# A new opening for a conditioned attention kernel: order of loads and transposes, and seven-product projections for batch 0

## The chip, the cores and the metric

The kernel runs on one core of a Trainium2 chip. A core has a matrix engine (TensorE, "PE" in the profile), a vector engine (VectorE, DVE), a scalar engine (ScalarE, ACT), GpSimd (POOL) and a queue engine (SyncE, SP). Each executes its own instructions in order; semaphores tie them together. Matmul results land in PSUM, which has eight banks of 128 partitions by 512 float32; all else is kept in SBUF. Data moves between memory and SBUF by DMA, issued here from SP and ACT.

The metric is the device time of one execution, in microseconds; less is better. "PEld" in the profile is the loading of a matmul's stationary operand, which overlaps other matmuls.

## The reference

Self-attention over `x` (8 batches, 512 rows, 512 columns, float32) with 16 heads of 32 columns. A condition row per batch goes through the Q and K projections too and is added to every row's Q and K. The result is added to `x`.

```python
Q = split_heads(x @ Wq.T + bq);  K = split_heads(x @ Wk.T + bk);  V = split_heads(x @ Wv.T + bv)
tQ = split_heads(tokens @ Wq.T + bq);  tK = split_heads(tokens @ Wk.T + bk)   # tokens = cond[:, None, :]
scores = einsum('bhqd,bhkd->bhqk', Q + tQ, K + tK) / sqrt(32)
attn = softmax(scores, axis=-1)
out = x + merge_heads(einsum('bhqk,bhkd->bhqd', attn, V))
```

All arithmetic is float32, and a float32 matmul shows in the trace as two passes (so four matmuls of a projection are listed as x8).

## The kernel before

**Tiling.** The four heads that share 128 columns form a *group*. There are four groups a batch and 32 in all, numbered `t` from 0. A group's Q and K are kept transposed, 128 columns (partitions) by 512 rows, in `qkT`. Rows come in four chunks of 128.

**Work on one group.** For each of four chunks, `row_max` makes the scores of the chunk's 128 rows for the four heads (`row_scores`, L419, into four banks), and DVE takes their maxima in two instructions (L428). `denominators` then lets ACT take the exponential of each of those four banks with the maximum as bias, and sum it (L456): four instructions. When all four chunks have their maxima, `split_max` (POOL) splits them into three bfloat16 parts and `transpose_max` turns them (L482). Only then `exponentials` makes the scores the other way round with the maxima subtracted by a matmul (L498, L501), and ACT writes the weights `e` (L513, L515). `weighted` multiplies them by V (L520), and `output` turns, divides and writes the result.

**The main loop** takes group `t` through four stages, one a chunk. In each stage PE does, in this order: the exponentials' matmuls of group `t`, the row scores of group `t + 1` or `t + 2`, and one piece of other work, among them half a projection for the next batch. It runs 29 times from L720; `advance` moves to the next row of `TURNS`, which says which bank each use has in each stage.

**Two ways to project.** `project_qk` makes one group's Q or K from the turned weight `wT` and the turned input `xT`: four matmuls of 128 by 512 (L255), then one instruction that adds the token's part `tok` and leaves PSUM (DVE for Q, L268; ACT for K, L270). `project_v` does a chunk of V (L281, L288). The other way makes two groups of Q or K, or half of V, at once by seven products of blocks instead of eight (`product`, L321 for V and L324 for Q and K; two matmuls of 128 by 256 each). It needs sums of blocks of the weights (`combine_w`, four POOL instructions for each weight) and of x (`combine_x`, two DVE instructions a half). It comes in halves: `first_products` (products 1, 6, one part of 2, 7) and `other_products` (4, 5, the rest of 2, 3). In `first_products`, product 1 and product 7 go to the two halves of one bank, `one_`, and 6 and 2 to another, `two_`; ACT copies product 1 out as `m1` (L357), and DVE forms sums from it (L364, L365, and `plus`, L344 or L347). The caller hands in `dens`, a function that issues denominators at a fixed place after m1's copy.

**Order.** PE, ACT, DVE and POOL execute in the order in which the program issues (`manual_schedule`); the framework adds the semaphores. DMA issues on SP are in order too. All of PSUM is one tile, cut into banks.

**The opening before.** SP issues the load of the condition, four chunks of x, then Wk, the two biases, the broadcast of bv, and Wv; ACT issues Wq's four chunks and then loads its function table. PE turns each chunk of x (`transpose_x`, L225) and of Wq (`transpose_w`, L180) in turn as they land, projects Q of group 0, does the condition's product for Q (`condition`, L591: product, ACT copy, L593), turns Wk, ends the condition (`condition_end`, L552: four transposes; DVE sums, L600 to L610), projects K of group 0 with the condition's K part inside, and turns half of Wv. Then five `burst_of_maxima` steps follow: row scores, maxima and denominators for a chunk, each with a projection behind it by `project_qk` or `project_v`. In the third to fifth of them the rest of Wv and the chunks of x of batch 1 are turned, and `combine_w` is issued. The projections of batch 0 left over go into the four stages of `t = 0`. So batch 0 is projected without the seven products, batches 1 to 7 with them.

Of the kernel before, what the change touches and what calls it, by code (L numbers as in the profile page):

```python
# [17 lines left out]
def kernel(  # L18
# [33 lines left out]
    nc = tc.nc  # L52
    P = 128
    B, S, D = x.shape
# [5 lines left out]
    NS = S // P  # L60
# [45 lines left out]
    def one():  # L106
        count[0] += 1
        return psum[:, (count[0] - 1) % 8, :]
# [1 line left out]

    xs = {}

    def load_x(n):

        if n < B * NS:
            xs[n] = xp.tile([P, D], F32, tag="x", name=f"x_{n}")
            nc.sync.dma_start(xs[n], x[n // NS, n % NS * P : (n % NS + 1) * P, :])

    xr = {}

# [8 lines left out]
        nc.gpsimd.tensor_tensor(xr[t], xr[t], bias, ALU.add)  # L129

    ws = {}
    for n in ("v", "q", "k"):
        ws[n] = stage.tile([P, NC, D], F32, tag="w", name=f"w_{n}")

    def load_w(n, w, queue):
        wv = w.rearrange("(c p) d -> p c d", p=P)
        for c in range(NC):
            queue.dma_start(ws[n][:, c, :], wv[:, c, :])

    cond_sb = const.tile([B, D], F32, tag="cond", name="cond_sb")  # L140
    nc.sync.dma_start(cond_sb, cond)
    for n in range(NS):
        load_x(n)
    load_w("q", Wq, nc.scalar)
    load_w("k", Wk, nc.sync)
    bqk = const.tile([P, 2, NC], F32, tag="bqk", name="bqk")
    nc.sync.dma_start(bqk[:, 0, :], bq.rearrange("(c p) -> p c", p=P))
    nc.sync.dma_start(bqk[:, 1, :], bk.rearrange("(c p) -> p c", p=P))
# [25 lines left out]
        n: const.tile([P, NC, D], F32, tag=f"wT{n}", name=f"wT_{n}") for n in ("q", "k", "v")  # L174
    }

    def transpose_w(n, dc, pt):

        for cc in range(NC):
            nc.tensor.transpose(  # L180
                pt[:, cc * P : (cc + 1) * P], ws[n][:, dc, cc * P : (cc + 1) * P], ident
            )
        o = wT[n][:, :, dc * P : (dc + 1) * P]
        pv = pt.rearrange("p (c s) -> p c s", c=NC)
        if n == "q":
            if dc % 2:
                nc.vector.tensor_scalar(o, pv, SCALE, None, ALU.mult)
            else:
                nc.scalar.activation(o, pv, AF.Copy, scale=SCALE)
        elif dc % 2:  # L190
            nc.vector.tensor_copy(o, pv)
        else:
            nc.scalar.copy(o, pv)
# [81 lines left out]
            project_qk_part(t, n, cc, pt)  # L275
        project_qk_end(t, n, pt)

    def project_v(n, pt):
        b, sc = divmod(n, NS)
        for cc in range(NC):  # L280
            nc.tensor.matmul(  # L281
                pt,
                xT[b][:, cc, sc * P : (sc + 1) * P],
                wT["v"][:, cc, :],
                start=(cc == 0),
                stop=(cc == NC - 1),
            )
        nc.vector.tensor_copy(vs[b % 2][:, sc, :], pt)  # L288

    MADE_OF = [("11", "11"), ("12", "21"), (3, "22"), ("22", 3), (0, 0), (1, 1), (2, 2)]
# [53 lines left out]
            add = tok[:, "qk".index(n), u * 2 + g, b : b + 1]  # L346
            nc.vector.scalar_tensor_tensor(o, pt, add, rest, ALU.add, ALU.add)  # L347

    def first_products(n, b, u, dens, small, at):

        one_, two_ = banks(0), banks(at)
        c1, c12, c2, c22 = parts_of(n, b, u)
        m1 = c2[:, 0, :]
        product(n, b, u, 1, one_[:, :HS])
        nc.scalar.copy(m1, one_[:, :HS])  # L357
        dens()
        small()
# [264 lines left out]
    warm = one()  # L624
    for _ in range(28):
        nc.tensor.matmul(warm[:, :P], onesb, onesb, start=True, stop=True)
    for c in range(NS):
        transpose_x(c, one())
        transpose_w("q", c, one())
        if c == 1:  # L630
            pc = one()
            for cc in range(NC):
                nc.tensor.transpose(
                    pc[:, cc * B : (cc + 1) * B], cond_sb[:, cc * P : (cc + 1) * P], ident[:B, :B]
                )
            nc.vector.tensor_copy(
                condT[:, :, 0:B], pc[:, : NC * B].rearrange("p (c b) -> p c b", b=B)
            )
    pq = one()
    for cc in range(NC):  # L640
        project_qk_part(0, "q", cc, pq)
    condition("q", one())
    for c in range(NC):
        transpose_w("k", c, one())
    condition_end("q", one())
    project_qk_end(0, "q", pq)
    condition("k", one())
    pk = one()
    for cc in range(NC):
        project_qk_part(0, "k", cc, pk)  # L650
        if cc == 1:
            condition_end("k", one())
    project_qk_end(0, "k", pk)
    transpose_w("v", 0, one())
    transpose_w("v", 1, one())
    turn[0] = 3

    def nothing():
        pass

    def burst_of_maxima(t, qc):
        row_max(t, qc)
        if qc == NS - 1:
            split_max(t)
        denominators(t, qc)

    burst_of_maxima(0, 0)
    project_qk(1, "q", banks(1))
    advance()
    burst_of_maxima(0, 1)  # L670
    project_qk(1, "k", banks(1))
    advance()
    burst_of_maxima(0, 2)
    transpose_w("v", 2, banks(0))
    transpose_w("v", 3, banks(1))
    transpose_x(NS, banks(2))
    project_qk(2, "q", banks(3))
    advance()
    burst_of_maxima(0, 3)
    for n in ("v", "q", "k"):  # L680
        combine_w(n)
    transpose_x(NS + 1, banks(0))
    project_v(0, banks(3))
    transpose_x(NS + 2, banks(1))
    project_qk(2, "k", banks(2))
    advance()
    burst_of_maxima(1, 0)
    project_v(1, banks(3))
    transpose_max(0, banks(1))
    transpose_x(NS + 3, banks(2))  # L690
    project_qk(3, "q", banks(0))
    load_residual(0)
    advance()

# [25 lines left out]
    for t in range(T - 3):  # L720
# [18 lines left out]
        exponentials(t, 1)  # L739
        row_max(t + 1, 2)  # L740
        denominators(t + 1, 2)
        if t:
            invert(t - 1, sums[t - 1])
# [172 lines left out]
```

## Time and profile before

| | |
|---|---|
| median of 3 runs | 767.25 us (766.59 to 768.86) |
| the profiled execution | 767.8 us, of which its span is 766.0 us |
| granted TensorE clock | 0.998 |
| first transposes of x on PE | 5.29 us |
| first projection (L255) | 10.22 us |
| first row scores (L419) | 24.10 us |
| first exponentials' matmul (L498) | 58.43 us |

The span runs from the program's first profiled instruction to its last; what lies around it, 1.8 us here, is in the time and not in the trace. PE is busy nearly throughout, so the profile is best read along PE: the chain of work that ended last names, step by step, what the next step waited for. The other engines matter only where they appear in it.

### The profile page before, as it was taken

Reading aid. Unit: us, or ns where it says so; the run is one execution under the profiler, and the core shown is the slowest. Engines: PE = TensorE matmul, PEld = TensorE weight load, DVE = VectorE, ACT = ScalarE, POOL = GpSimd, SP = SyncE. Lnnn points to the kernel's source line nnn. Section 1 sums busy time; section 2 is a strip of 40 time slices with the busy share of each in tenths; the row PEclk is TensorE's granted clock in tenths of the full one; section 3 lists DMA queues with packets and bytes.
Section 4 is the critical chain, followed back from the end, with each engine's and each line's share of the span. In section 5 each row is a group of like instructions: output and inputs, shape, how many; then the busy total and the mean of one; then the engine's idle time right before and its main releaser. Section 6 shows DMA issues by size and latency. Waiting matters only on the chain.

```text
span 766.0 us, 14203 instructions
## 1 busy us (share of the span) xinstructions
PE 754.7 (99%) x5424; PEld 426.3 (56%) x5424; DVE 521.5 (68%) x720; ACT 627.1 (82%) x1454; POOL 127.3 (17%) x223
## 2 busy tenths in 40 slices
PE   8999999999999999999999999999999999999997
PEld 5444566555656655555655555665555665555332
DVE  4455676676767777677777776777766777667664
ACT  2447898888889888888888888898888988888865
POOL 0063011111011111111111101111110111110220
PEclk9999999999999999999999999999999999999999
DMA  9011011101111110111111011110101101010100
GB/s 305 26 42 29 15 42 42 32 12 45 40 43 42 40 31 15 42 42 43 42 28 43 15 42 42 42 42 11 46 1 29 29 29 28 1 39 18 43 28 28
DMA packets 41571, 29.76 MB, mean 39 GB/s; under 512 B 2840, under 2 KB 35608, under 8 KB 41504
## 3 DMA queue, kind: packets, MB, share of 16 engines
q1 hardware_dynamic: 40656, 27.68, 12.7%
q10 hardware_dynamic: 848, 1.18, 0.5%
q8 instruction: 42, 0.69, 0.4%
q14 instruction: 25, 0.20, 0.1%
HBM read 20.47 MB, written 8.39 MB: 38 GB/s over the span
## 4 chain that ended last, share of the span: by engine, by line
PE 96%; ACT 1%; DVE 1%; DMA 1%; issue 0%; SPq 0%; DVEq 0%
PE psum L324 23%; PE psum L520 15%; PE psum L501 14%; PE psum L419 14%; PE psum L321 12%; PE psum L498 6%; PE psum L255 4%; PE psum L225 2%; PE psum L552 2%; PE psum L281 2%; PE psum L482 1%; DMA x<-in_x_dram 1%; ACT e L513 1%; PE psum L180 1%; ACT e L515 0%
## 5 line engine op out<-in xcount | busy, mean ns | idle before, releaser
L428 DVE TENSOR_REDUCE nmax<-psum 128x2 f32<-128x1024 f32 x256 | 301.7, 1219 | 165.0 <-PE psum L419 164.0
L456 ACT ACTIVATE dead<-psum,nmax 128x512 f32<-128x512 f32 x496 | 335.0, 692 | 23.1 <-DVE nmax L428 23.1
L513 ACT ACTIVATE e<-psum 128x512 f32<-128x512 f32 x270 | 145.8, 595 | 86.6 <-PE psum L501 86.6
L419 PE MATMUL psum<-kT,qT 32*128 32x512 f32 x1024 | 138.9, 598 | 0.3 <-ACT e L515 0.3
L501 PE MATMUL psum<-qT,kT 32*128 32x512 f32 x1024 | 132.7, 589 | 0.0
L515 ACT ACTIVATE e<-psum 128x1024 f32<-128x1024 f32 x121 | 124.7, 1031 | 0.0
L520 PE MATMUL psum<-e,v 128*32 128x512 f32 x1024 | 119.0, 598 | 0.4 <-ACT e L515 0.3
L456 ACT ACTIVATION_READ_ACCUMULATOR dead<-psum,nmax 128x1 f32 x496 | 103.6, 209 | 0.0
L470 POOL CAST split<-nmax 128x16 bf16<-128x16 f32 x32 | 8.2, 255 | 544.2 <-DVE nmax L428 544.2
L419 PEld LDWEIGHTS psum<-kT,qT 32*128 32x128 f32 x1024 | 64.7, 183 | 52.0 <-issue 27.7
L520 PEld LDWEIGHTS psum<-e,v 128*32 128x32 f32 x1024 | 29.6, 110 | 83.2 <-issue 58.2
L498 PE MATMUL psum<-maxT,onesb 3*128 3x512 bf16 x512 | 51.2, 384 | 1.7 <-DVE res L566 0.8
L501 PEld LDWEIGHTS psum<-qT,kT 32*128 32x128 f32 x1024 | 51.1, 185 | 2.5 <-issue 0.2
L577 POOL TENSOR_TENSOR res<-res,xr 128x512 f32<-128x512 f32 x30 | 38.2, 1272 | 66.1 <-DVE res L566 66.1
L498 PEld LDWEIGHTS <-onesb 3*128 3x128 bf16 x512 | 13.3, 91 | 63.6 <-issue 54.1
L542 DVE COPY oT<-psum 128x512 f32<-128x512 f32 x29 | 20.0, 691 | 35.7 <-PE psum L520 35.7
L324 PE MATMUL psum<-xc,wc_q 128*128 128x256 f32 x168 | 43.4, 380 | 0.3 <-ACT e L515 0.3
L321 PE MATMUL psum<-wc_v,xc 128*128 128x256 f32 x168 | 43.2, 380 | 0.0
L324 PE MATMUL psum<-xc,wc_k 128*128 128x256 f32 x168 | 43.2, 380 | 0.0
L129 POOL TENSOR_TENSOR xr<-xr,bvb 128x512 f32<-128x512 f32 x32 | 40.6, 1269 | 0.0
L324 PEld LDWEIGHTS psum<-xT,wT_k 128*128 128x128 f32 x168 | 26.4, 190 | 12.8 <-ACT e L513 10.6
L324 PEld LDWEIGHTS psum<-xc,wc_q 128*128 128x128 f32 x168 | 30.8, 190 | 4.7 <-ACT e L515 1.1
(144 smaller groups left out, 834.1 us busy)
## 6 DMA issues: line engine op xcount, KB each, us to landing
x<-in_x_dram SPq DMA_DIRECT2D x33, 256.0 KB, 2.7
xr<-in_x_dram SPq DMA_DIRECT2D x32, 256.0 KB, 3.1
out_dram<-res SPq DMA_DIRECT2D x31, 256.0 KB, 2.4
w_q<-in_L_cond_Wq_dram ACTq DMA_DIRECT2D x4, 256.0 KB, 4.5
w_k<-in_L_cond_Wk_dram SPq DMA_DIRECT2D x4, 256.0 KB, 4.9
w_v<-in_L_cond_Wv_dram SPq DMA_DIRECT2D x4, 256.0 KB, 6.7
bvb<-in_L_cond_bv_dram SPq DMA_DIRECT2D x1, 256.0 KB, 6.2
out_dram<-res SPq DMA_DIRECT2D x1, 128.0 KB, 1.8
```

Of the source, the lines that this page charges most:

```text
L129: nc.gpsimd.tensor_tensor(xr[t], xr[t], bias, ALU.add)
L321: nc.tensor.matmul(pt, xb, w, start=(kc == kcs[0]), stop=(kc == kcs[-1]))
L324: nc.tensor.matmul(pt, w, xb, start=(kc == kcs[0]), stop=(kc == kcs[-1]))
L419: nc.tensor.matmul(pt, qkT["q", t][r, qc * P : (qc + 1) * P], qkT["k", t][r, :], start=True, stop=True,)
L428: nc.vector.tensor_reduce(nmax[t][:, qc, pr * 2 : pr * 2 + 2, 0], pt, AX.X, ALU.max, negate=True)
L456: nc.scalar.activation(dead, banks(HG + j), AF.Exp, bias=nmax[t][:, qc, j, :], accum_out=sums[t][:, qc, j, :],)
L498: nc.tensor.matmul(bank[j], onesb[r, :], maxT[t][r, :], start=True, stop=False)
L501: nc.tensor.matmul(bank[j], qkT["k", t][r, kc * P : (kc + 1) * P], qkT["q", t][r, :], start=False, stop=True,)
L513: nc.scalar.activation(e[:, i, :], bank[pr * 2 + i], AF.Exp)
L515: nc.scalar.activation(e, banks(2, 2), AF.Exp)
L520: nc.tensor.matmul(pt[j * HD : (j + 1) * HD, :], vs[b % 2][:, kc, (g * HG + j) * HD : (g * HG + j + 1) * HD], es[t, kc, j // 2][:, j % 2, ...
L577: last.tensor_tensor(y, y, xr.pop(t), ALU.add)
```

## The change

It touches the opening, the five burst steps and the four stages of `t = 0`. Nothing else in the kernel is changed.

- Loads: SP issues x_0, Wq's first chunk, x_2, Wq's other chunks, then the condition, the biases, bv's broadcast and Wv. ACT issues x_1, x_3 and Wk's four chunks.
- Transposes: all four chunks of x and the first chunks of Wq and Wk come first, with the two projections of group 0 between them; x's copies out of PSUM alternate between DVE and ACT. `combine_x` for batch 0 follows the Q projection. The other chunks of Wq and Wk come next, then the condition's whole work for both, and all of Wv. `combine_w` is issued as each weight is complete.
- Bursts: the turning of batch 1's chunks of x, and the transposed maxima, go between the maxima and the denominators, with ACT copying. `split_max(0)` moves behind the fourth burst.
- Projections: Q, K of groups 0 and 1 stay as they were; groups 2 and 3 and all of V of batch 0 use `first_products` and `other_products`. `project_v` goes. In the bursts the products come after `denominators` with nothing handed in as `dens`.

```diff
-    def load_x(n):
+    def load_x(n, queue=nc.sync):
...
-    for n in ("v", "q", "k"):
+    for n in ("q", "k", "v"):
         ws[n] = stage.tile([P, NC, D], F32, tag="w", name=f"w_{n}")
...
+    load_x(0)
+    load_x(1, nc.scalar)
+    load_w("q", Wq, nc.sync, [0])
+    load_x(2)
+    load_x(3, nc.scalar)
+    load_w("k", Wk, nc.scalar, [0])
+    load_w("q", Wq, nc.sync, [1, 2, 3])
+    load_w("k", Wk, nc.scalar, [1, 2, 3])
     cond_sb = const.tile([B, D], F32, tag="cond", name="cond_sb")
     nc.sync.dma_start(cond_sb, cond)
-    for n in range(NS):
-        load_x(n)
-    load_w("q", Wq, nc.scalar)
-    load_w("k", Wk, nc.sync)
...
-    def first_products(n, b, u, dens, small, at):
+    def first_products(n, b, u, dens, small, at, first=0):
...
-        one_, two_ = banks(0), banks(at)
+        one_, two_ = banks(first), banks(at)
...
-    for c in range(NS):
-        transpose_x(c, one())
-        transpose_w("q", c, one())
...
-    pq = one()
+    for c, copy in ((0, nc.vector.tensor_copy), (1, nc.scalar.copy)):
+        transpose_x(c, one(), copy)
+    transpose_w("q", 0, one(), 1)
+    for c, copy in ((3, nc.scalar.copy), (2, nc.vector.tensor_copy)):
+        transpose_x(c, one(), copy)
+    pq, pk = one(), one()
+    one_of = [0]
+
+    def other():
+        one_of[0] += 1
+        return psum[:, (one_of[0] - 1) % 5, :]
+
     for cc in range(NC):
         project_qk_part(0, "q", cc, pq)
-    condition("q", one())
-    for c in range(NC):
-        transpose_w("k", c, one())
-    condition_end("q", one())
-    project_qk_end(0, "q", pq)
-    condition("k", one())
-    pk = one()
+    transpose_w("k", 0, other(), 0)
+    combine_x(0, 0)
+    combine_x(0, 1)
     for cc in range(NC):
         project_qk_part(0, "k", cc, pk)
-        if cc == 1:
-            condition_end("k", one())
+    for n in ("q", "k"):
+        for c in range(1, NC):
+            transpose_w(n, c, other(), (c + (n == "k")) % 2)
+        combine_w(n)
+    pc = other()
...
+    condition("q", other())
+    condition("k", other())
+    transpose_w("v", 0, other())
+    transpose_w("v", 1, other())
+    condition_end("q", other())
+    project_qk_end(0, "q", pq)
+    condition_end("k", other())
     project_qk_end(0, "k", pk)
-    transpose_w("v", 0, one())
-    transpose_w("v", 1, one())
+    transpose_w("v", 2, other())
+    transpose_w("v", 3, other())
+    combine_w("v")
     turn[0] = 3
...
-    def burst_of_maxima(t, qc):
+    def burst_of_maxima(t, qc, between=nothing):
+
         row_max(t, qc)
-        if qc == NS - 1:
-            split_max(t)
+        between()
         denominators(t, qc)
 
-    burst_of_maxima(0, 0)
+    burst_of_maxima(0, 0, lambda: transpose_x(NS, banks(0), nc.scalar.copy))
     project_qk(1, "q", banks(1))
     advance()
-    burst_of_maxima(0, 1)
+    burst_of_maxima(0, 1, lambda: transpose_x(NS + 1, banks(0), nc.scalar.copy))
     project_qk(1, "k", banks(1))
     advance()
-    burst_of_maxima(0, 2)
-    transpose_w("v", 2, banks(0))
-    transpose_w("v", 3, banks(1))
-    transpose_x(NS, banks(2))
-    project_qk(2, "q", banks(3))
+    burst_of_maxima(0, 2, lambda: transpose_x(NS + 2, banks(0), nc.scalar.copy))
+    first_products("q", 0, 1, nothing, nothing, 3, 2)
     advance()
     burst_of_maxima(0, 3)
-    for n in ("v", "q", "k"):
-        combine_w(n)
-    transpose_x(NS + 1, banks(0))
-    project_v(0, banks(3))
-    transpose_x(NS + 2, banks(1))
-    project_qk(2, "k", banks(2))
+    split_max(0)
+    other_products("q", 0, 1, nothing, nothing, (0, 3))
+    first_products("v", 0, 0, nothing, nothing, 2, 1)
     advance()
-    burst_of_maxima(1, 0)
-    project_v(1, banks(3))
-    transpose_max(0, banks(1))
-    transpose_x(NS + 3, banks(2))
-    project_qk(3, "q", banks(0))
+    burst_of_maxima(1, 0, lambda: transpose_max(0, banks(2), nc.scalar.copy))
+    first_products("k", 0, 1, nothing, nothing, 1, 3)
+    other_products("v", 0, 0, nothing, nothing, (0, 2))
     load_residual(0)
     advance()
...
-                dens()
-                project_qk(3, "k", banks(1))
+                other_products("k", 0, 1, dens, nothing, (1, 3))
...
-            project_v(2, banks(0))
+            first_products("v", 0, 1, dens, nothing, 1)
...
-            dens()
-            project_v(3, banks(0))
+            other_products("v", 0, 1, dens, nothing, (0, 2))
```

`transpose_w` gets an argument that picks the engine of its copy (DVE if odd, else ACT), and `load_w` one that picks chunks.

More of the change, by code (lines that the diff above doesn't have):

```diff
@@ L111 @@
     xs = {}
-    def load_x(n):
+    def load_x(n, queue=nc.sync):
         if n < B * NS:
             xs[n] = xp.tile([P, D], F32, tag="x", name=f"x_{n}")
-            nc.sync.dma_start(xs[n], x[n // NS, n % NS * P : (n % NS + 1) * P, :])
+            queue.dma_start(xs[n], x[n // NS, n % NS * P : (n % NS + 1) * P, :])
     xr = {}
@@ L131, with load_w @@
     ws = {}
-    for n in ("v", "q", "k"):
+    for n in ("q", "k", "v"):
         ws[n] = stage.tile([P, NC, D], F32, tag="w", name=f"w_{n}")
-    def load_w(n, w, queue):
+    def load_w(n, w, queue, cs=range(NC)):
         wv = w.rearrange("(c p) d -> p c d", p=P)
-        for c in range(NC):
+        for c in cs:
             queue.dma_start(ws[n][:, c, :], wv[:, c, :])
+    load_x(0)
[6 more added lines that the diff above has]
+    load_w("k", Wk, nc.scalar, [1, 2, 3])
     cond_sb = const.tile([B, D], F32, tag="cond", name="cond_sb")
     nc.sync.dma_start(cond_sb, cond)
-    for n in range(NS):
-        load_x(n)
-    load_w("q", Wq, nc.scalar)
-    load_w("k", Wk, nc.sync)
     bqk = const.tile([P, 2, NC], F32, tag="bqk", name="bqk")
@@ L175, with transpose_w @@
     }
-    def transpose_w(n, dc, pt):
+    def transpose_w(n, dc, pt, odd=None):
+        odd = dc % 2 if odd is None else odd
         for cc in range(NC):
@@ L185, in transpose_w @@
         if n == "q":
-            if dc % 2:
+            if odd:
                 nc.vector.tensor_scalar(o, pv, SCALE, None, ALU.mult)
@@ L189, in transpose_w @@
                 nc.scalar.activation(o, pv, AF.Copy, scale=SCALE)
-        elif dc % 2:
+        elif odd:
             nc.vector.tensor_copy(o, pv)
@@ L276, in project_qk @@
         project_qk_end(t, n, pt)
[L278 to L288, printed above, removed]
     MADE_OF = [("11", "11"), ("12", "21"), (3, "22"), ("22", 3), (0, 0), (1, 1), (2, 2)]
@@ L626 @@
         nc.tensor.matmul(warm[:, :P], onesb, onesb, start=True, stop=True)
-    for c in range(NS):
-        transpose_x(c, one())
-        transpose_w("q", c, one())
[L630 to L638, printed above, removed]
-    pq = one()
+    for c, copy in ((0, nc.vector.tensor_copy), (1, nc.scalar.copy)):
[8 more added lines that the diff above has]
+        return psum[:, (one_of[0] - 1) % 5, :]
     for cc in range(NC):
         project_qk_part(0, "q", cc, pq)
-    condition("q", one())
-    for c in range(NC):
-        transpose_w("k", c, one())
-    condition_end("q", one())
-    project_qk_end(0, "q", pq)
-    condition("k", one())
-    pk = one()
+    transpose_w("k", 0, other(), 0)
+    combine_x(0, 0)
+    combine_x(0, 1)
     for cc in range(NC):
         project_qk_part(0, "k", cc, pk)
-        if cc == 1:
-            condition_end("k", one())
+    for n in ("q", "k"):
[3 more added lines that the diff above has]
+    pc = other()
+    for cc in range(NC):
+        nc.tensor.transpose(
+            pc[:, cc * B : (cc + 1) * B], cond_sb[:, cc * P : (cc + 1) * P], ident[:B, :B]
+        )
+    nc.vector.tensor_copy(condT[:, :, 0:B], pc[:, : NC * B].rearrange("p (c b) -> p c b", b=B))
+    condition("q", other())
[5 more added lines that the diff above has]
+    condition_end("k", other())
     project_qk_end(0, "k", pk)
-    transpose_w("v", 0, one())
-    transpose_w("v", 1, one())
+    transpose_w("v", 2, other())
+    transpose_w("v", 3, other())
+    combine_w("v")
     turn[0] = 3
@@ L740 @@
         row_max(t + 1, 2)
-        denominators(t + 1, 2)
+        dens = lambda: denominators(t + 1, 2)
         if t:
+            dens()
             invert(t - 1, sums[t - 1])
```

## The prediction

> **What bounds the kernel now.** I read the page's totals, then the chain that ended last in order of time, then each engine's timeline of the first 100 us. Totals and chain shares:
>
> ```profile
> PE 754.7 (99%) x5424; PEld 426.3 (56%) x5424; DVE 521.5 (68%) x720; ACT 627.1 (82%) x1454; POOL 127.3 (17%) x223
> ...
> PE 96%; ACT 1%; DVE 1%; DMA 1%; issue 0%; SPq 0%; DVEq 0%
> ```
>
> TensorE's own order sets the end. What is cut there, or added as a wait there, moves the end one for one; all else is free until it makes PE wait. The chain in order of time (start, length, what) over the part that changes:
>
> ```profile
> 10.22 3.67 PE psum L255 x8
> ...
> 18.35 0.76 DVE qT L268
> 19.11 0.04 issue
> 19.15 1.98 PE psum L255 x4
> ...
> 24.17 1.50 PE psum L419 x7
> ...
> 58.50 0.33 PE psum L498 x4
> ...
> 75.93 0.33 PE psum L498 x4
> ```
>
> So: first projection 10.22, first row scores (L419) 24.17, first exponentials (L498) 58.50, fourth stage of group 0 75.93. From there on both programs do the same, so the sum is three stretches: up to 24.17, 34.33 us to 58.50, 17.43 us to 75.93.
>
> **Stretch 1: the opening.** Loads first. Queue issues (start, length):
>
> ```profile
> 0.73 1.84 ACTq L138 DMA_DIRECT2D w_q<-in_L_cond_Wq_dram  x4
> ...
> 0.74 0.40 SPq L141 DMA_DIRECT2D cond_sb<-in_cond_dram  x1
> 1.20 2.71 SPq L117 DMA_DIRECT2D x<-in_x_dram  x4
> ...
> 2.60 1.28 ACT L189 ACT_TABLE_LOAD   x1 [2.60 <-issue]
> ```
>
> Queried one by one, x_2 (third on SP, issued 2.05) landed 5.7 later, at 7.75. Now cond's 0.4 issue ahead of x is gone, and x_2 is still third: about 7.3 (between 6.5, where the third of ACT's loads landed, and 7.75). Moving the other loads (Wq behind x on SP, cond, biases, Wv last) costs nothing while they land before use: Wv landed by 18.6, and is now used at 22.6; without that cover the delay would be one for one. Batch 1's x still queues behind Wv on SP: its last landed at 21.4, the first is used at 28.4.
>
> ACT now issues six loads, not four, ahead of its table load. The rows show issues being held: x_3's came 1.1 us after x_2's ended, at 3.58, just as the oldest load landed (0.73+2.8), and bk's at 8.02 as Wq's last landed (2.1+5.9). Eight loads were in flight each time. I read: a ninth waits for the oldest. ACT's fifth and sixth issues then wait for two of the first four loads; the fourth to land before did so at 6.2, less the head start about 5.9. So ACT is free at 5.9+0.45, has its table at 7.6, and has copied x_1 and x_3 (0.60 each) at 8.8; first projection 8.9. Bounds: no hold, and x_2's landing decides (7.3+0.45 transposes+0.1+0.70 copy = 8.6); held on x_2, 7.3+0.45+1.28+1.2 = 10.3. I take 8.9, since the rows show the oldest load deciding.
>
> From there PE's order: q projection 3.67 to 12.6; Wk's first four transposes 0.44; ACT copy 0.59 with 0.1 either side, PE idle, to 13.8; k projection 3.63 to 17.45; six sets of transposes 6x0.44 to 20.1; cond's transposes 0.41 and copy 0.18 with hand-overs, to 20.75; both condition products 1.00+0.86 (chain and L591 rows) to 22.6; two sets of Wv 0.88 to 23.5; DVE's copy of the second to 24.3. Then a chain that formerly ran beside the k projection lies bare. By the old rows: sum_q to qT 0.85 (17.50 to 18.35), qT 0.67, sum_k to tok 0.74 (21.69 to 22.43), hand-over 0.06, kT to first scores 0.76: 3.08, so scores start at 27.3. PE fills it with two transpositions of partial sums and the rest of Wv (4x0.44), done at 25.3, and idles 2.0. **Term: +3.15**, of which 0.88 is Wv work brought forward. Cut at nothing: combine_x, 4x0.69 on DVE, lies under the q projection (without that cover up to 2.8); combine_w, 12x1.27 = 15.2 on POOL from 20, is done by 35, before V's first product of sums at about 49.
>
> **Stretch 2: five bursts.** Work first. A projection in the chain is 3.44 (3.63 behind scores); seven products replace two:
>
> ```profile
> 83.67 1.06 PE psum L324 x4
> 84.73 0.44 PE psum L225 x4
> 85.17 2.16 PE psum L324 x10
> ...
> 106.62 3.02 PE psum L324 x14
> ```
>
> Half of seven products is 3.02 to 3.22 against 3.44. For eight projections over both stretches the bare work falls from 8x3.44 = 27.5 to 28x0.86 = 24.1: 3.4 less. But the new first halves are issued behind `denominators`, whereas the main loop puts m1's copy ahead of them. The order on ACT is now four denominators, then m1. And the seventh product goes into the bank that m1 is read from (`one_`, other half). That halves of one bank are kept apart shows at the end of the kernel:
>
> ```profile
> 760.38 0.42 DVE L858 COPY oT<-psum 128x256 f32<-128x256 f32 x1 [2.34 <-PE psum L520]
> 760.84 0.37 ACT L859 COPY oT<-psum 128x256 f32<-128x256 f32 x1 [0.73 <-DVE oT L858]
> ```
>
> Both only read disjoint columns of one bank, yet ACT waits for DVE. So product 7 waits for m1. From the start of the scores: maxima +1.2 (29.23 to 30.60 is the old worst, 1.37), first exponential +1.26 (30.60 to 31.86), four of them 2.66 (31.86 to 34.52), m1 0.37, hand-over 0.1: product 7 at +5.6. PE is there much earlier:
>
> - q's first half: 0.95 scores, 0.58 transposes of x, 0.86+0.86+0.43 products: +3.7. Stall 1.9.
> - k's first half: 0.95, 0.25 maxima, 1.06+0.86+0.22: +3.35. Stall 2.2.
> - V's first half comes after q's second half (3.2), which covers it: none.
>
> The steps: 1.05+0.58+3.44 = 5.1; 0.95+0.58+3.44 = 5.0; 5.6+0.86 = 6.45; 0.95+3.2+3.1 = 7.25; 5.6+0.86+3.2 = 9.65. Sum 33.4 against 34.33. The x transposes now lie between scores and projection, so ACT's banks come free in time (the old scores took 1.28 and 1.62 there); their copies go to ACT ahead of the exponentials, in its wait for the maxima (2.47 idle): nothing. POOL's remainder copy and split follow work long done. DVE loses V's plain copies (0.69 each) and gains sums of 0.41 to 0.75, in time it idles (1.05 to 3.68 before the maxima): nothing, unless a sum delays maxima. **Term: -0.95.** Bounds: -4.9 (no stall), +0.5 (0.2 to 0.3 more at each of five hand-overs).
>
> The Trainium skill, "PSUM — Partial Sum Buffer", section "PSUM bank collisions raise a hardware error", says to guard PSUM by bank and not by address; it speaks against this order as the two rows do. By that rule the stalls stand; by columns alone the change would win about 2.9.
>
> **Stretch 3: group 0.** Stages as in the main loop: k's second half with x transposes 5.65 (103.99 to 109.64, q's) plus 0.22; V's first 2.05+3.22 = 5.27; V's second 5.55-0.22 = 5.33. Sum 16.47 against 17.43: **-0.96.** ACT's load there is 2.03+2.66+0.37 = 5.1 a stage, just under PE's, so no more is to be had; if it decided, some 0.5 is lost.
>
> **Sum:** +3.15-0.95-0.96 = +1.24. The profiled execution took 767.8 (span 766.0 and 1.8 around it): 769.0. The median of the runs is 0.55 lower: 768.4.
>
> The granted clock is 1.00 in every us of the opening, PE's 0.9 of idle before 5.29 included. The skill's "TensorE: Matmul & The Clock Gate", Part 1, halves the clock after an idle window of about 3.4 us; by it the new idles of 2 cost nothing extra, and one that filled a window would add an estimated 1.7. No run here shows either.
>
> **Rivals.**
>
> 1. *Halves are kept apart by columns where PE writes.* The two rows are of two readers; PE against ACT isn't shown. Then 4.1 of stalls go: 1.24-4.1 = -2.9, 764.4. For it: PE is in order and the columns are disjoint. Against: the rows, and V's first sum at 80.87, which starts only after the next product in the same bank.
> 2. *Slower: ACT's own issues hold it.* If the sixth waits for x_2 and not for an older load, table load and both copies end at 10.3, and all of PE's order follows one for one: +1.4, 1.24+1.4 = +2.6, 769.9. It decides once x_3's copy ends after 8.9. For it: the two held SP issues. Against: both waited for the oldest load.
> 3. *No net change: the opening pays its way.* If DVE is free of Wv's copy and the bare chain is covered, the 2.0 idle shrinks to about 0.6: 1.24-1.4 = -0.2, 767.1. Against: the old rows leave 3.08 serial.
>
> **How the numbers follow.** A measurement tells 0.3%, 2.3 us, from no change. Forecast 52% (own range 766.3 to 770.6; 10 points of it beyond 769.5), rival 1 12% (9 faster), rival 2 22% (15 slower), rival 3 14% (1 faster). Faster 10%, same 65%, slower 25%. Leaving a tenth out at each end gives 765.0 to 771.0: low takes in rival 3 and what is short of rival 1, high rival 2 with the 0.5 of stretch 3 and some stall.
>
> **What would show it.** First L255 near 8.9 and ACT's table load ending near 7.6; first L419 near 27.3 with PE idle before it; two PE waits of about 2 us ahead of the seventh products of q and k, released by ACT; first L498 33.4 after the first L419, fourth 16.5 later. No such waits means rival 1; a table load ending at 9 means rival 2; scores before 26 means rival 3. Anything different after the fourth L498 would make the prediction's frame wrong.

## The result, and the profile after

The changed kernel takes **777.6 us** (median of 5 runs, 777.16 to 779.51) against 767.41 (5 runs, 766.59 to 768.86) for the kernel before: a ratio of 1.0129, 95% interval 1.0109 to 1.0149. It is slower by 10 us, outside the predicted range of 765.0 to 771.0; 768.4 was forecast. The profiled execution has a span of 775.3 us and a mean granted clock of 0.993.

The page's totals and the shares of the chain of waits, changed kernel:

```profile
PE 753.8 (97%) x5472; PEld 437.7 (56%) x5472; DVE 530.9 (68%) x735; ACT 630.2 (81%) x1462; POOL 127.7 (16%) x224
...
PE 94%; ACT 2%; DVE 2%; DMA 1%; issue 1%; ACTq 0%; DVEq 0%
```

PE's busy time is about what it was (754.7 before), but its share of the chain fell from 96% to 94%, and ACT and DVE gained a point each. So the time went into waits of PE more than into work. The chain in order of time shows where (start, length, what; changed kernel, its first 90 us):

```profile
2.13 6.38 DMA x<-in_x_dram
...
10.52 5.20 PE psum L261 x8
...
33.61 2.55 PE psum L413 x8
36.15 1.04 PE psum L231 x4
...
69.88 0.33 PE psum L492 x4
...
86.43 0.33 PE psum L492 x4
```

L261 is the projection, L413 the row scores and L492 the exponentials' first matmul (L255, L419 and L498 before). The three stretches of the prediction, from these lines:

| stretch | before | predicted | after | after less before |
|---|---|---|---|---|
| to the first row scores | 24.17 | 27.3 | 33.61 | +9.44 |
| to the first exponentials | 34.33 | 33.4 | 36.27 | +1.94 |
| to the fourth stage of group 0 | 17.43 | 16.47 | 16.55 | -0.88 |
| sum | 75.93 | 77.17 | 86.43 | +10.50 |

After the fourth stage the two traces run 10.50 us apart throughout the main loop. Only at the very end 1.2 us are made up, and by no merit of the change: the profile of before has a stretch at half clock there (725.2 to 728.6) that the other one hasn't. So the whole loss is made in the opening, and the second stretch, forecast as a gain, is a small loss.

**The first stretch** is 6.3 us over its forecast, and the lines split it. The first projection starts at 10.52, not 8.9: 1.6. It takes 5.20, not 3.67: 1.5. From the start of DVE's chain for the condition (27.50) to the scores it takes 6.11, not 3.08: 3.0. That leaves 0.1.

For the late start, the issues and ACT's instructions (changed kernel, timeline: start, length, engine):

```profile
0.73 0.41 ACTq L117 DMA_DIRECT2D x<-in_x_dram  x1
1.17 0.93 ACTq L138 DMA_DIRECT2D w_k<-in_L_cond_Wk_dram  x2
2.13 0.45 ACTq L117 DMA_DIRECT2D x<-in_x_dram  x1
4.60 1.58 ACTq L138 DMA_DIRECT2D w_k<-in_L_cond_Wk_dram  x2
6.21 1.28 ACT L234 ACT_TABLE_LOAD   x1 [6.21 <-DMA w_k<-in_L_cond_Wk_dram]
```

ACT's issues are held, as the prediction read from the page, and the table is ready at 7.49 (forecast 7.6). But x_3, which the program issues second on ACT, went out fourth, behind two chunks of Wk, and landed at 8.51. The opening's loads stand outside the part with a hand-written order, and there the framework chose another one.

For the long projection, windows of the same kernel (stretch, its length, then busy time and instructions of PE, PEld, DVE, ACT, POOL; granted clock; DMA share; GB/s):

```profile
6.80:10.20 3.40, 1.41 (x11) 0.93 (x9) 1.21 (x2) 1.86 (x3) 0.00 (x0) 1.00 1.05 387
10.20:13.60 3.40, 3.08 (x4) 1.52 (x5) 2.76 (x5) 0.00 (x0) 0.00 (x0) 0.50 1.10 288
27.30:30.70 3.40, 1.24 (x12) 1.00 (x10) 3.30 (x6) 0.00 (x0) 3.32 (x4) 0.99 0.00 0
30.70:34.10 3.40, 0.49 (x4) 0.49 (x7) 2.66 (x5) 1.16 (x2) 2.08 (x2) 0.50 0.00 0
34.10:37.50 3.40, 3.40 (x13) 1.73 (x11) 1.77 (x2) 0.27 (x1) 3.32 (x3) 0.50 0.00 0
```

The granted clock is 0.50 in three stretches of 3.4 us, and each time the stretch ahead was thinly used: PE was busy 1.41, 1.24 and 0.49 of 3.4 us. The first such stretch covers most of the Q projection. The third covers the first burst's scores (2.55 us) and transposes (1.04). The first burst takes 7.23 us and not 5.1, which is 2.1 of the 2.9 us that the second stretch is over its forecast. Not all of that is the clock: the first scores took 1.50 in the kernel before too, at full clock, where the prediction set 1.05.

For the chain on DVE, first DVE's timeline of the changed kernel:

```profile
27.70 1.29 DVE L601 TENSOR_SCALAR bqk<-bqk 128x4 f32<-128x4 f32 x1
...
29.25 1.14 DVE L604 TENSOR_TENSOR tok<-sum_q,bqk 128x32 f32<-128x32 f32 x1
30.43 0.75 DVE L274 TENSOR_SCALAR qT<-psum,tok 128x512 f32<-128x512 f32 x1
31.65 1.19 DVE L604 TENSOR_TENSOR tok<-sum_k,bqk 128x32 f32<-128x32 f32 x1
```

Then POOL's at the same time, `combine_w` of K:

```profile
27.69 1.27 POOL L215 TENSOR_TENSOR wc_k<-wT_k 128x512 f32<-128x512 f32 x1
29.04 1.30 POOL L216 TENSOR_TENSOR wc_k<-wc_k,wT_k 128x512 f32<-128x512 f32 x1
...
31.53 1.25 POOL L218 TENSOR_TENSOR wc_k<-wT_k,wc_k 128x512 f32<-128x512 f32 x1
```

Three of the chain's five instructions of 4 and 32 columns, which took 0.16 to 0.19 us before, take 1.14 to 1.29. Each of the three starts beside a POOL instruction and ends with it: L601 with L215 (28.99 and 28.96), the first L604 with L216 (30.39 and 30.34), the second with L218 (32.84 and 32.78). The copies out of PSUM between them (L274) keep their length.

**The two stalls** of the second stretch stand where they were forecast (PE's timeline, changed kernel; in brackets the idle time before and what ended it):

```profile
51.80 1.10 PE L318 MATMUL psum<-xc,wc_q 128*128 128x256 f32 x4 [1.78 <-ACT qT L351]
65.73 1.13 PE L318 MATMUL psum<-xc,wc_k 128*128 128x256 f32 x4 [2.12 <-ACT kT L351]
```

### The profile page after: what moved, and what is told of

It reads as the page before. It is cut to its first block, busy times and chain, and to the rows that moved or that the text cites. A ratio compares the mean times of both kernels' runs of the same rounds, so it can differ in the third digit from the quotient of the medians.

```text
span 775.3 us, 14337 instructions
## 1 busy us (share of the span) xinstructions
PE 753.8 (97%) x5472; PEld 437.7 (56%) x5472; DVE 530.9 (68%) x735; ACT 630.2 (81%) x1462; POOL 127.7 (16%) x224
## 4 chain that ended last, share of the span: by engine, by line
PE 94%; DVE 2%; ACT 2%; DMA 1%; issue 1%; ACTq 0%; DVEq 0%
PE psum L318 24%; PE psum L514 15%; PE psum L495 14%; PE psum L413 14%; PE psum L315 13%; PE psum L492 6%; PE psum L261 2%; PE psum L231 2%; PE psum L546 2%; DVE nmax L422 1%; PE psum L476 1%; DMA x<-in_x_dram 1%; ACT dead L450 1%; ACT e L507 1%; PE psum L186 0%
## 5 line engine op out<-in xcount | busy, mean ns | idle before, releaser
L413 PE MATMUL psum<-kT,qT 32*128 32x512 f32 x1024 | 138.6, 599 | 5.4 <-ACT kT L276 5.1
L413 PEld LDWEIGHTS psum<-kT,qT 32*128 32x128 f32 x1024 | 64.6, 184 | 55.8 <-issue 28.2
L492 PE MATMUL psum<-maxT,onesb 3*128 3x512 bf16 x512 | 51.3, 384 | 2.1 <-DVE maxT L482 1.1
L315 PE MATMUL psum<-wc_v,xc 128*128 128x256 f32 x192 | 49.4, 380 | 0.0
L571 POOL TENSOR_TENSOR res<-res,xr 128x512 f32<-128x512 f32 x30 | 38.1, 1270 | 66.2 <-DVE res L560 66.2
L492 PEld LDWEIGHTS <-onesb 3*128 3x128 bf16 x512 | 13.4, 91 | 62.5 <-issue 52.9
L318 PE MATMUL psum<-xc,wc_q 128*128 128x256 f32 x180 | 46.5, 381 | 2.1 <-ACT qT L351 1.8
L318 PE MATMUL psum<-xc,wc_k 128*128 128x256 f32 x180 | 46.4, 380 | 2.1 <-ACT kT L351 2.1
L315 PEld LDWEIGHTS psum<-wc_v,xc 128*128 128x128 f32 x192 | 35.4, 190 | 4.3
L315 PE MATMUL psum<-wT_v,xT 128*128 128x256 f32 x128 | 37.8, 397 | 0.0
```

The source lines that it names most:

```text
L315: nc.tensor.matmul(pt, xb, w, start=(kc == kcs[0]), stop=(kc == kcs[-1]))
L318: nc.tensor.matmul(pt, w, xb, start=(kc == kcs[0]), stop=(kc == kcs[-1]))
L413: nc.tensor.matmul(pt, qkT["q", t][r, qc * P : (qc + 1) * P], qkT["k", t][r, :], start=True, stop=True,)
L492: nc.tensor.matmul(bank[j], onesb[r, :], maxT[t][r, :], start=True, stop=False)
L571: last.tensor_tensor(y, y, xr.pop(t), ALU.add)
```

## The experiments

The theory after the result had three parts in the opening (POOL's additions beside DVE's chain, the order of loads, the granted clock) and one in the bursts (m1 behind the denominators, in the bank of product 7). E1 to E4 undo one each, E5 treats the clock, E6 puts POOL's cost into the kernel before, and E7 to E12 combine. Ratios are to the kernel before, run beside them.

| | kernel | median us | ratio (95%) |
|---|---|---|---|
| E1 | changed, `combine_w` later | 777.81 | 1.0126 (1.0102 to 1.0150) |
| E2 | changed, loads in written order | 775.92 | 1.0110 (1.0090 to 1.0129) |
| E3 | changed, m1 ahead of denominators | 775.35 | 1.0101 (1.0086 to 1.0116) |
| E4 | changed, product 7 in another bank | 775.23 | 1.0094 (1.0077 to 1.0112) |
| E5 | changed, PE kept busy | 775.25 | 1.0077 (1.0053 to 1.0102) |
| E6 | before, POOL beside its chain | 772.38 | 1.0044 (1.0026 to 1.0061) |
| E7 | E1 + E2 + E3 | 768.29 | 1.0005 (0.9987 to 1.0023) |
| E8 | old opening, new bursts, m1 first | 765.52 | 0.9963 (0.9949 to 0.9978) |
| E9 | E7 + E5 | 769.82 | 1.0018 (1.0005 to 1.0031) |
| E10 | E8, rest of Wv in the third burst | 763.93 | 0.9947 (0.9928 to 0.9966) |
| E11 | E1 + E5 | 773.40 | 1.0068 (1.0052 to 1.0084) |
| E12 | old opening, bursts as the change has them | 768.95 | 1.0012 (0.9999 to 1.0025) |

### E1: POOL's additions behind the condition's chain

```diff
         for c in range(1, NC):
             transpose_w(n, c, other(), (c + (n == "k")) % 2)
-        combine_w(n)
...
     condition_end("k", other())
+    gate = const.tile([P, NC, B], F32, tag="gate", name="gate")
+    nc.gpsimd.tensor_copy(gate, tok[:, 1])
+    combine_w("q")
+    combine_w("k")
```

POOL's copy of `tok` waits for the chain's last result, so the additions can't run beside it.

> The changed kernel with the weight sums of Q and K held back on POOL until the condition's K part is done (a small POOL copy of tok ahead of them); all else as it was. Theory A (DVE instructions with SBUF operands wait while a POOL instruction runs): the three long DVE instructions of the bias chain (1.29, 1.14, 1.19 us) go back to 0.16 to 0.19, first row scores 3.0 earlier (33.6 to about 30.6), and since PE then idles 2 us and not 5, the clock stays at 1.00 and the first burst step falls from 7.2 to about 5.1: 777.6 - 5 = 772.5 (771.5 to 773.5). Rival B (they are long for another reason, the scattered bias loads or semaphores): nothing moves, 777 to 778.

Measured: 777.81, no gain. DVE's timeline of E1 shows that the mechanism itself was right:

```profile
28.87 0.16 DVE L601 TENSOR_SCALAR bqk<-bqk 128x4 f32<-128x4 f32 x1
...
29.29 0.19 DVE L604 TENSOR_TENSOR tok<-sum_q,bqk 128x32 f32<-128x32 f32 x1
...
30.73 0.19 DVE L604 TENSOR_TENSOR tok<-sum_k,bqk 128x32 f32<-128x32 f32 x1
```

From the chain's start (28.67) to the scores (31.69) it is now 3.02 us, which is the 3.08 of the prediction. What took the gain away is in E1's windows (columns as above):

```profile
28.80:32.20 3.40, 1.41 (x13) 1.01 (x14) 2.54 (x9) 1.16 (x2) 1.22 (x2) 1.00 0.00 0
32.20:35.60 3.40, 3.40 (x13) 1.68 (x8) 2.29 (x2) 0.31 (x1) 3.32 (x4) 0.51 0.00 0
35.60:39.10 3.50, 3.50 (x5) 1.35 (x4) 0.07 (x1) 2.96 (x9) 3.42 (x4) 0.51 0.29 75
...
49.30:52.70 3.40, 1.61 (x11) 0.86 (x9) 0.90 (x3) 2.15 (x7) 0.00 (x0) 1.00 0.14 54
52.70:56.10 3.40, 3.40 (x12) 1.63 (x13) 1.89 (x3) 0.08 (x1) 0.00 (x0) 0.50 0.02 5
```

In the profile of the changed kernel one of the three stretches at half clock fell mostly on idle time, where it cost next to nothing. In E1's there are five: two at the start (8.3 to 15.2), two over the first burst, where PE has work, and one behind the first stall. The idle time just before the scores is 1.99 us, and the clock fell all the same: the expectation had it back at 1.00 with 2 us of idle time, and that is the part of it that failed. The rival had the three instructions keep their length, and they did not. E1's four executions run from 774.9 us at a mean clock of 0.993 to 778.6 at 0.989, and the profiled one is of the long ones.

### E2: the loads in the order that the program writes

```diff
-    load_x(0)
-    load_x(1, nc.scalar)
+    with tc.manual_schedule(engines={mybir.EngineType.Activation, mybir.EngineType.SP}):
+        load_x(0)
+        load_x(1, nc.scalar)
...
```

> The changed kernel with its opening loads kept in the order in which they are written, so that ACT issues x_3 second and not fourth; all else as it was. Theory A (x_3's late landing starts the Q projection late, and the idle before it halves PE's clock): x_3 lands at about 6, ACT's copies end at 8.8, Q projection from 8.9 in 3.67 us instead of 5.20; all behind it 3.1 earlier: 774.5 (774 to 775.5). Rival B (the long projection is not of the idle, but of traffic or of operands): only the 1.6 of the start, 776.

Measured: 775.92, 1.4 above the expectation and 0.19% below the changed kernel. The Q projection starts at 9.49 and takes 3.70 us at a granted clock of 1.00. The start is later than the prediction's 8.9 by 0.6. ACT's timeline of E2 shows why:

```profile
1.66 5.38 ACTq L138 DMA_DIRECT2D w_k<-in_L_cond_Wk_dram  x4
7.07 1.28 ACT L235 ACT_TABLE_LOAD   x1 [7.07 <-DMA x<-in_x_dram]
```

The last of ACT's six issues goes out at 6.71, just as x_2 lands (issued 1.65, landed 5.04 later), and the table load follows it. That is the hold of the prediction's rival 2, at a smaller price, 9.49 and not 10.3, since x_2 landed at 6.69 and not at 7.3. Up to the scores 2.5 us are gained (31.08 against 33.61), but 0.8 of that is lost in the first burst, which takes 8.00 against 7.23 (E2's windows):

```profile
26.30:29.70 3.40, 0.00 (x0) 0.00 (x0) 3.23 (x7) 0.00 (x0) 3.32 (x4) 1.00 0.00 0
29.70:33.10 3.40, 2.02 (x8) 0.97 (x8) 1.21 (x2) 1.16 (x2) 2.00 (x3) 0.50 0.00 0
33.10:36.50 3.40, 3.40 (x11) 1.91 (x8) 2.36 (x2) 1.79 (x5) 3.40 (x3) 0.50 0.19 45
```

With PE a little earlier and DVE's chain still slow, PE idles a whole stretch, and the next two are at half clock.

### E3 and E4: the two stalls

E3 puts m1's copy ahead of the denominators, as the main loop does:

```diff
-    burst_of_maxima(0, 2, lambda: transpose_x(NS + 2, banks(0), nc.scalar.copy))
-    first_products("q", 0, 1, nothing, nothing, 3, 2)
+    row_max(0, 2)
+    transpose_x(NS + 2, banks(0), nc.scalar.copy)
+    first_products("q", 0, 1, lambda: denominators(0, 2), nothing, 3, 2)
```

and the same for K's half in the fifth burst.

> The changed kernel with ACT's copy of m1 ahead of the denominators in the third and fifth burst (the denominators handed in, as the main loop does); all else as it was. Theory A (product 7 waits for m1, which stood behind four exponentials): the waits of 1.78 and 2.12 on PE go; the next scores may then wait some tenths for the exponentials: 777.6 - 3.5 = 774.1 (773.7 to 775.5). Rival B (the exponentials' rate bounds these steps anyway, so the wait only moves to the next row scores): 776.5 to 777.6.

E4 leaves ACT's order and gives product 7 another bank:

```diff
-        product(n, b, u, 7, one_[:, HS:])
+        seventh = one_[:, HS:] if seven is None else banks(seven)[:, HS:]
+        product(n, b, u, 7, seventh)
```

> The changed kernel with product 7 of these two halves put in a bank of its own; ACT's order stays, m1 behind the denominators. Theory A (what holds product 7 is only that m1 is being read from the other half of its bank): both waits ahead of product 7 go; K's may come back in part (about 0.9) where V's second half needs that bank: 777.6 - 3 = 774.6 (774 to 775.6). Rival B (product 7 is held by something else that m1's copy releases): both waits stay, 777 to 778.

Measured: 775.35 and 775.23, both within 1.3 us of what was expected. Both waits before product 7 are gone in both. What is late next, in PE's timeline of E3, is the row scores of the fourth burst, which need the bank that the last denominator reads:

```profile
50.97 1.80 PE L413 MATMUL psum<-kT,qT 32*128 32x512 f32 x8 [0.32 <-ACT dead L450]
```

In E4 K's product 7 follows at once, and a quarter of the wait comes back where V's second half needs the bank:

```profile
67.08 0.70 PE L315 MATMUL psum<-wT_v,xT 128*128 128x256 f32 x2 [0.58 <-DVE kT L341]
```

E4 decides against the prediction's rival 1: the columns were disjoint all the time, and only the change of the bank removed the wait. Whether the chip needs that wait, or only the framework's semaphores keep the halves apart, no run shows.

### E5: PE kept busy through the opening's waits

```diff
     transpose_w("q", 0, one(), 1)
+    for _ in range(12):
+        nc.tensor.matmul(warm[:, :P], ones, ones, start=True, stop=True)
...
         transpose_x(c, one(), copy)
+    for _ in range(6):
+        nc.tensor.matmul(warm[:, :P], ones, ones, start=True, stop=True)
...
     combine_w("v")
+    for _ in range(4):
+        nc.tensor.matmul(psum[:, 5, :], ones, wT["q"][:, 0, :], start=True, stop=True)
```

The added matmuls are read by nobody.

> The changed kernel with idle PE time filled by matmuls whose result nobody reads: 12 small ones after Wq's first transposes, 6 after x_2's, and 4 of 512 columns in the gap before the first row scores. No dependence is changed. Theory A (the clock is halved by the idle before): the Q projection takes 3.67 and not 5.20, the first burst step about 5.1 and not 7.2, clock 1.00 throughout: 777.6 - 3.6 = 774.0 (773.5 to 775). Rival B (these stretches are long for another reason): no gain, 777.5 or a little more.

Measured: 775.25, just above what was expected, with a ratio of 1.0077 against 1.0129. PE's timeline of E5:

```profile
6.11 2.84 PE L625 MATMUL psum<-ones 128*128 128x128 f32 x24
...
11.00 3.60 PE L261 MATMUL psum<-xT,wT_q 128*128 128x512 f32 x8
```

The projection is at full clock (3.60, not 5.20) and so is the first burst (5.55 us, not 7.2), though nothing was taken off any engine. So low use of PE, not the data or the instructions, lengthened both; of the first burst's 2.1 us it was 1.6. The mean clock is 0.997 to 1.000 in E5's four executions and 0.991 to 0.993 in the five of the changed kernel. E3's trace says the same from the other side: with the opening of the changed kernel unaltered, the two stretches ahead of 11.3 are used 1.60 and 1.86 of 3.4 us, the clock stays at 1.00, and the Q projection takes 3.67. So where a stretch falls differs between executions of one opening. E5's clock is not at 1.00 throughout, as was expected: behind K's stall, at 63.2, a stretch at half clock is left. The added work cost something itself: the first twelve take 2.84 us and push the projection to 11.00.

### E6: the same load on POOL in the kernel before

```diff
         transpose_w("k", c, one())
+    spare = const.tile([P, D], F32, tag="spare", name="spare")
+    for i in range(10):
+        nc.gpsimd.tensor_tensor(spare, wT["q"][:, i % 4, :], wT["q"][:, (i + 1) % 4, :], ALU.add)
     condition_end("q", one())
```

> The kernel before, with ten POOL additions of 128x512 into a tile that nobody reads, beside its bias chain (about 11 to 24 us). Theory A (SBUF-to-SBUF work on DVE waits while a POOL instruction runs): the DVE instructions of the bias chain that read SBUF go from 0.16 to 0.19 to as much as 1.3, the first row scores come 1.5 to 3 later than 24.1, DVE's copies out of PSUM stay at 0.69: 767.4 + 1.5 to 3.5. Rival B: POOL's work costs DVE nothing, 767.4.

Measured: 772.38, which is 1.5 above the range expected. DVE's timeline of E6:

```profile
18.52 1.18 DVE L607 TENSOR_SCALAR bqk<-bqk 128x4 f32<-128x4 f32 x1
19.73 0.19 DVE L609 TENSOR_TENSOR sum_q<-sum_q,bqk 128x32 f32<-128x32 f32 x1
19.96 1.14 DVE L610 TENSOR_TENSOR tok<-sum_q,bqk 128x32 f32<-128x32 f32 x1
...
26.21 0.19 DVE L610 TENSOR_TENSOR tok<-sum_k,bqk 128x32 f32<-128x32 f32 x1
```

POOL's ten additions run from 11.65 to 25.08. Of the three small DVE instructions on SBUF inside that time two take 1.18 and 1.14. The third, L609, takes 0.19: it starts at 19.73, just ahead of POOL's next instruction (19.75). The one behind POOL's work takes 0.19 too; nothing else was changed. This is the mechanism by itself. The first scores came 4.5 us later (28.57): 0.8 was there at the first projection already (11.04 against 10.22), ahead of POOL's work, 2.0 are the two instructions, and 1.7 a stretch at half clock that followed here too (23.0 to 26.4). The runs show the same split: three of the ten executions, at a mean clock of 1.000, took 768.9 to 769.6, the other seven, at 0.993 to 0.996, 771.5 to 773.8.

### E7, E9 and E11: the repairs together

E7 is E1, E2 and E3 in one kernel.

> The changed kernel with three edits together: weight sums on POOL after the bias chain, loads as written, m1 ahead of the denominators. Theory A (three separate losses, which add): first row scores at about 27.3 as the prediction had it, bursts 29.5 to 30.5, group 0 16.5: 73.3 to 74.3 against 75.9 before, so 764.8 to 765.8, faster than the kernel before. Rival B (the losses overlap, or the new opening has another): 767 or more.

E9 is E7 with E5's added matmuls, the last four cut to two; E11 is E1 with the same.

> The kernel with the three edits, and idle PE time filled in the opening. Theory A (what is left above the prediction's sum is the halved clock: its profile showed three stretches of 3.4 us of it in the opening): Q projection 3.67 and not 5.40, first burst step about 5.1 and not 8.9; 768.3 - 4 = 764.3 (763.5 to 766), and less scatter between runs. Rival B (the clock is not what is left): 767.5 to 768.5.

> The kernel with idle PE time filled, and the weight sums of Q and K held back as well (two fillers of 512 columns instead of four ahead of the first row scores, since that gap is now 2 us). Theory A (the sums held back gained nothing alone because two more stretches of half clock ate the 3.1 us; with PE kept busy the gain shows): first row scores 3 earlier than in the kernel with fillers alone, 775.3 - 3 = 772.3 (771.5 to 773). Rival B (the bias chain is hidden behind something else): 775 or more.

Measured: 768.29, 769.82 and 773.40; all three short of what was expected, E7 and E9 by more than 2 us. E11 against E5 repeats E1's comparison with the clock held up: from the start of the first projection to the first scores 18.4 us against 21.5, so 3.1 less. The fourth stage of group 0 starts 2.4 us earlier (82.93 against 85.34) and the median is 1.9 lower, but the two ratios' intervals overlap, so how much of the 3.1 reaches the end isn't settled. E11's profile has one stretch at half clock behind the stall that it kept, at 61.1.

E7's three edits save 1.24% together, but 0.03%, 0.19% and 0.28% alone: a sum of 0.50%. Its profiled execution, the slowest of its 12 runs, still has the Q projection and the projection of the first burst at half clock (chain of E7):

```profile
9.59 5.40 PE psum L262 x8
...
33.38 5.34 PE psum L262 x8
```

E9's has both at full clock, with the added matmuls (L626) ahead of the first (chain of E9):

```profile
6.25 2.68 PE psum L626 x24
...
11.14 3.44 PE psum L262 x8
...
31.57 3.44 PE psum L262 x8
```

From the start of the first projection to the fourth stage of group 0 E9 needs 66.2 us and E7 71.3, so 5.1 less. But the added matmuls moved that start from 9.59 to 10.98, and E9's median is not below E7's. Even so repaired, the new opening reaches its first scores at 29.4 against 24.1 in the kernel before, and E9 gains nothing (1.0018, 1.0005 to 1.0031).

### E8, E12 and E10: the old opening with the new bursts

E8 takes the kernel before up to the first row scores, with `combine_x` of batch 0 on DVE behind the transposes of x and `combine_w` behind a gate as in E1, and then the change's bursts and stages of group 0, with m1 first as in E3. Wv's last two chunks are turned in the second burst. E12 is the same with the bursts as the change has them.

> The old opening (its loads and its order up to the first row scores) with the new bursts and seven products, m1 ahead of the denominators, the weight sums after the bias chain, and the last two sets of Wv turned in the second burst. Theory A (the gain is in the products, and all that the new opening brings is a loss): first row scores at 24.2 as before, bursts 30 to 31, group 0 16.5: 71 to 72 against 75.9, so 762.5 to 763.5. Rival B (the new opening is needed for the products' gain): no faster than the other kernel of this call with three edits.

> The old opening with the bursts as the change has them: m1's copy behind the denominators (and the last two sets of Wv turned in the second burst). Theory A (the opening is the whole of the loss, and the bursts even as they stand about break even): 765.5 + 2.7 = 768.2 (767.5 to 769), that is some 9 to 10 less than the changed kernel, with the two waits ahead of product 7 there again. Rival B (much of the loss is in the bursts): 771 or more.

Measured: 765.52 and 768.95. E12 is the change without its opening, and stands at +0.12% where the change stands at +1.29%: the new opening costs 1.17%, 9.0 us. Both waits ahead of product 7 are there in E12 (1.55 and 2.12). The bursts and products, as written, gain nothing that can be measured (0.9999 to 1.0025), and with m1 first they gain 0.37%. E8's expectation was 2 to 3 us too good. Its chain of waits shows one wait that is left:

```profile
40.18 2.13 ACT dead L446 x6
```

The fourth burst's scores (L409) wait for ACT's denominators, as in E3. E10 moves the turning of Wv's chunks out of the second burst and into this wait, behind Q's first half, and lets ACT make both copies:

```diff
-    transpose_w("v", 2, banks(2))
-    transpose_w("v", 3, banks(3))
-    combine_w("v")
     advance()
...
     first_products("q", 0, 1, lambda: denominators(0, 2), nothing, 3, 2)
+    transpose_w("v", 2, banks(1), 0)
+    transpose_w("v", 3, banks(4), 0)
+    combine_w("v")
```

> The old opening with the new bursts, and the last two sets of Wv turned in the third burst behind Q's first half, where PE waited 2.1 us for the exponentials, instead of in the second; both copied by ACT. Theory A (that wait hides them): second burst 5.1 instead of 6.0, third no longer than 6.0: 765.5 - 0.9 = 764.6. Rival B (their copies delay the exponentials and so the next scores by as much): 765.5.

Measured: **763.93** (6 runs, 762.57 to 765.71), ratio 0.9947 (0.9928 to 0.9966): faster than both kernels. Against E8 the intervals overlap; in the profiles the second burst takes 5.10 us and not 5.96, and the third, with the chunks in it, 5.81 and not 5.91. The chain of E10, where no wait is left between the row scores' and the exponentials' starts:

```profile
24.28 1.50 PE psum L409 x7
...
36.81 3.02 PE psum L314 x14
39.84 0.87 PE psum L182 x8
40.71 1.25 PE psum L409 x8
...
55.50 0.33 PE psum L488 x4
...
72.04 0.33 PE psum L488 x4
```

From the first scores to the first exponentials it is 31.2 us against 34.33 before, and to the fourth stage another 16.5 against 17.43. Together that is 4.0 us less, with the old opening's 24.2 kept. So the seven products and the reordered transposes of the bursts gain once no wait stands in them.

## Why the prediction was wrong

**Loads: issues are held, as the prediction read, but the order was wrong.** The table was there at 7.49, with 7.6 forecast. That was luck in part: it came so in an order of loads that the prediction didn't have, and in the order that it took from the diff (E2) the table is there at 8.35 and the start is 9.49. So 0.6 of the 1.6 us was the estimate of the hold, by x_2 as rival 2 had it, and the other 1.0 the order: x_3 went out fourth, and its landing decided.

**The step that failed first: "combine_w ... is done by 35", costed at nothing.** It was timed against its reader, V's sums, and not against what runs beside it. The prediction itself had laid the condition's chain bare on DVE, and put POOL's 15 us from 20 on across it. Cost: 3.0 us, shown by E1 (the chain is back at 3.02) and by itself in E6. The Trainium skill, "SBUF — State Buffer", section "Who interferes with whom", states that a DVE instruction with two SBUF inputs contends with a GpSimd instruction that reads SBUF, and that whichever is first holds the other off for a whole instruction. The runs agree for the additions: 0.19 became 1.14 to 1.19, beside POOL instructions of 1.25 to 1.30. The scaling of bq (L601, L607 in E6), which has one SBUF input, is not covered by that sentence and took 1.29 and 1.18 all the same.

**The step that failed second: "the new idles of 2 cost nothing extra".** In the profiled execution the clock took 1.5 us from the Q projection and 1.6 from the first burst. E5, which only kept PE busy, brought both back to full clock. The rule that the prediction leaned on is "TensorE: Matmul & The Clock Gate", Part 1, of the Trainium skill: half clock after an idle window of about 3.4 us. The grain agrees, as stretches at half clock are 3.4 us or multiples of it. The condition does not: PE was busy 1.41 of 3.40 us ahead of the stretch at 10.2, and in E1 1.41 and 1.61 ahead of 32.2 and 52.7, and no idle piece there was as long as 3.4. The measurement decides, and a forecast has to look at how full each window is, not at the longest idle piece, though the share alone does not decide it either (see what stays open).

**The bare chain** of 3.08 us, with PE idle 2.0, was right in kind and size: E1 has 3.02 and 1.99.

**Bursts: right but for the clock.** The stalls of 1.9 and 2.2 were 1.78 and 2.12, by m1's copy as said. The steps of 5.1, 5.0, 6.45, 7.25 and 9.65 came out at 7.23, 5.10, 6.96, 7.31 and 9.67; the first is 1.6 of half clock, and 0.5 of first scores set too low. Without the new opening, the stages' gain of 0.96 is there (in E12 16.54 us against 17.43 before), but the bursts' 0.95 is not: 37.55 against 34.33. Some 0.9 of that is Wv's turning, which the change has in its opening; the last step takes 11.36 and not 9.65, with a stretch at half clock behind K's stall (56.0 to 59.4). A stall can thus be dearer than its length. E3 and E4 show two ways out, worth 0.28% and 0.35% by their medians.

**Group 0's stages:** 16.47 forecast, 16.55 measured.

**Rivals.** Rival 1 (apart by columns) falls with E4. Rival 2's hold is there in the written order (E2) but didn't decide the changed kernel. Rival 3 fails, since the scores came later and not earlier. The rivals were all variations of one chain of PE, ACT and transfers; none let two engines that share no data slow each other.

**What stays open.** What exactly the clock goes by: a stretch with PE busy 2.26 of 3.40 us (721.8 to 725.2 of the kernel before) was followed by half clock, while one of E2 with 1.59 of 3.40 (5.8 to 9.2) was not. How much of the 9.0 us the clock takes in an execution other than the profiled one isn't seen stretch by stretch. It moves with where idle time falls, which may be why the repairs didn't add up (E7, 1.24% against 0.50%). What the repaired opening is worth at full clock can be read from E7's executions: the three with a mean clock of 1.000 took 766.5 to 766.7. The kernel before, run beside them, took 766.7 to 767.5 in nine of ten executions at 0.999 or 1.000 (770.3 in the other), and E8, with the old opening, 764.4 to 764.9 in three. So even then the new opening only breaks even, and is some 2 us behind the old one with the same products.

## What to carry to other kernels

Before an instruction is costed at nothing because its result is needed late, look at what runs beside it: here POOL's additions on SBUF stretched tiny DVE instructions on SBUF to about the length of a POOL instruction, and three of these in a chain cost 3 us. Thin stretches of PE can be paid twice, once as idle time and once at half clock in the work behind, so an opening that starts its first product earlier but leaves holes (E2, 9.49) can lose to one that starts late and stays dense (10.22). And read the order of loads from a trace or force it; where the framework schedules, the program's order is only a wish.

## What the runs showed of the hardware that was not expected

- DVE beside POOL: 128x4 and 128x32 float32 instructions on SBUF, when they started up to 0.2 us behind a POOL addition, took 1.14 to 1.29 us instead of 0.16 to 0.19; copies from PSUM (L274, 0.75) did not change.
- The granted clock fell to 0.50 after stretches of 3.4 us in which PE was busy 1.2 to 1.6 us (the idle piece before the scores of E1 was 1.99 us), though not after every such stretch: 1.46 and 1.59 in E2 and 1.60 in E3 left it at 1.00.
- A stretch at half clock in which PE was busy throughout (3.40 of 3.40, E1 at 32.2) did not bring the clock back; the next one was still at 0.51. In the changed kernel one like it (34.1 to 37.5) did.
